# Three reorderings in a two-layer kernel: a copy ahead of the down scalings, weight sums in the order of the text, and one zero matmul fewer at the start

## The chip, the core and the metric

The kernel runs on one core of one Trainium2 chip. The metric is the device time of one execution in microseconds (us). A core has five engines with a queue of instructions each: TensorE (matmuls; PE in the profile, PEld for its weight loads), VectorE (DVE), ScalarE (ACT), GpSimd (POOL) and SyncE (SP), which here only issues DMAs. They wait for each other through semaphores.

## The reference, cut to what matters

```python
# x: (8, 256, 1024) f32; mask: (8, 1024, 1024) int32; coeff: (8,); W: (1024, 1024)
def first(x, W, b, coeff, mask):
    sign = 2 * mask - 1
    return einsum('bsi,oi->bso', x, W) + b + einsum('bsi,bio->bso', x, sign) * coeff[:, None, None]

def second(x, mapping, W, b, lora_As, lora_Bs):        # rank 16, SCALING = 2
    A, Bm = lora_As[mapping], lora_Bs[mapping]
    return einsum('bti,oi->bto', x, W) + b + einsum('btr,bro->bto', einsum('bti,bir->btr', x, A), Bm) * SCALING

x = x + first(x, W0, b0, coeff, mask)
x = x + second(x, W1, b1, mapping, lora_As, lora_Bs)
```

Every batch of the first layer has a weight of its own, W0 + coeff (2 mask - 1), and both residuals are put into the weights as an identity.

## The kernel before

Everything is held transposed: features on the 128 partitions, the 256 tokens of a batch along the free axis, in float32. The eight batches form two groups of four; each group goes through the first layer batch by batch and then through the second layer at once.

**Start.** `c_row`, the eight coefficients, is loaded by ScalarE's queue (L90). `idle(n)` (L98 to L100) issues n matmuls of zeros, which compute nothing that is used. `idle(2)` stands ahead of `spread` (L104), a matmul that copies the coefficients to all partitions (`c_ps`); `idle(3)` stands behind it. VectorE makes `two_c` and `neg_c` from `c_ps` (L108, L110). A float32 matmul shows as two matmuls in the profile.

**First layer.** A piece of mask is loaded by SyncE, ScalarE turns it into coeff (2 mask - 1) (`build`, L237) and VectorE adds W0 (L245). Batch 0 (L303) and batches 1 and 2 (L278) are plain products. Batches 3 to 7 (class `Seven`) multiply by blocks with seven products instead of eight (the Strassen-Winograd scheme): `token_sum` (L373) makes the sums t1 to t4 of the tokens, `weight_sum` (L356) the sums s1 to s4 of the weight blocks, each in two halves a = 0 and 1, `half` (L420) issues one half of a product, `with_bias` (L439, ScalarE) and `add` (L446, VectorE) read the results. For batch 3 the sums s3 and s4 are written over a weight block that has no other use left; other batches have a buffer for them. `operands` gives the order of the sums in the text: for each half s1 and then s2, then t3, s3, s4, t4. `products` gives the order of TensorE: X (a11), Y (a12), X (s2 with t2), Z (s1 with t1), X (s3 with t3), Z (s4), X (a22 with t4).

**Second layer.** The same seven-product scheme on two levels: `second_layer` runs seven outer products (`plan`), each of seven inner products (`product`, L722) whose weight operands ("leaves", `l_...`) are loaded by SyncE from DRAM, where GpSimd's queue has put them (`keep`, L534). `read` takes a product out of PSUM: ScalarE copies it (L776) where nothing is added, VectorE adds it (L778). The first outer product, `run(0, "A11", ...)`, has the adapters beside it: after its first two inner products `down` issues 64 small matmuls into `psh` (L757) and ScalarE scales the four batches' rows into `h_sb` (L766); later `up` multiplies `h_sb` by the adapters' rows into `G` (L740), which ScalarE copies (L750).

In group 0 the weight sums of the outer product S3 are made beside this: GpSimd's queue loads eight blocks again (`again`, L616), VectorE subtracts them (`outer`, L608) and makes the inner sums later (`inner_in_place`, L597).

**What sets the order.** A scheduler puts the instructions of each engine into an order of its own; the order of the text is only a wish. `tc.issue_after(i)` holds whatever is issued inside it behind instruction i. `behind(what)` does so with the last instruction that was noted in `anchors` under that name, and does nothing when none was noted. No order is given in `weight_sum` among the sums, nor in `down` between the scalings and the copy that `read` issues just ahead of it in the text.

Of the kernel before, what the change touches and what calls it, by code (L numbers as in the profile page):

```python
# [20 lines left out]
SCALING = 2.0  # L21
# [3 lines left out]
def kernel(  # L25
# [38 lines left out]
    nc = tc.nc  # L64
    B, NG, _, _, T = xT.shape
    R = lora_b.shape[1]
# [4 lines left out]
    GB = 4  # L71
    NGROUP = B // GB
    S = 32
# [21 lines left out]
    h_sb = const.tile([P, T], F32, tag="h", name="h_sb")  # L95
    idle_ps = psum.tile([P, T], F32, tag="ps", name="idle_ps")

    def idle(n: int):  # L98
        for _ in range(n):
            nc.tensor.matmul(idle_ps, lhsT=zeros[:, :P], rhs=zeros, start=True, stop=True)  # L100

    idle(2)
    c_ps = psum.tile([P, B], F32, tag="ps", name="c_ps")
    spread = nc.tensor.matmul(c_ps, lhsT=one_row, rhs=c_row, start=True, stop=True)  # L104
    with tc.issue_after(spread.ins):
# [31 lines left out]
    anchors = {}  # L137
# [6 lines left out]
    def behind(what: str):  # L144
        return tc.issue_after(anchors[what].ins) if what in anchors else nullcontext()
# [114 lines left out]
    def bank(name):  # L260
        return psum.tile([P, 2, T], F32, tag="ps", name=name)
# [67 lines left out]
    class Seven:  # L329
# [19 lines left out]
        def weight_sum(self, n, op, x, y, a):  # L349

            if self.b < GB and n in ("s3", "s4"):
                s = self.w[x, a]
            else:
                s = qpool.tile([P, CG, OH], F32, tag="q", name=f"{n}_{self.b}_{a}")
            self.w[n, a] = s
            anchors["weights"] = op(s, self.w[x, a], self.w[y, a])  # L356

        def tokens(self, c, v):

# [335 lines left out]
    def second_layer(group: int, y, first, first_steps, second):  # L695
# [3 lines left out]
        a = la_of[group]  # L699
# [52 lines left out]
        def down():  # L752
            ph = bank(f"psh_{group}")
            with behind("inner"):
                for c in range(NC):
                    for i in range(GB):
                        anchors["adapters"] = nc.tensor.matmul(  # L757
                            ph[i * S : i * S + R, 0, :],
                            lhsT=a[:, i, c, :],
                            rhs=y[i][c // TPH][:, c % TPH, :],  # L760
                            start=(c == 0),
                            stop=(c == NC - 1),
                        )
            for i in range(GB):
                rows = slice(i * S, i * S + R)
                nc.scalar.mul(h_sb[rows, :], ph[rows, 0, :], SCALING)  # L766

        banks = {}

# [142 lines left out]
        for _ in chain(islice(s3, 1), ordered(second.sums()), islice(t1, 2)):  # L912
# [4 lines left out]
            0, "A11", first, None, e1,  # L917
            beside=islice(s3, 4),
            early=down,
            mid=lambda: up(0, 0, lower),  # L920
            late=lambda: up(0, 1, lower),
# [67 lines left out]
    sums = iter(())  # L989
# [13 lines left out]
    for group in range(NGROUP):  # L1003
        y = [
            [
                ypool.tile([P, TPH, T], F32, tag=f"y{i}{h}", name=f"y_{GB * group + i}_{h}")
                for h in range(2)
            ]
            for i in range(GB)
        ]  # L1010
# [113 lines left out]
```

## Time and profile before

| what | value |
|---|---|
| three runs | 410.59, 412.04, 412.46 us (median 412.04) |
| profiled execution | 411.16 us, of which the span of instructions 409.5 us |
| granted TensorE clock | 1.00 of full speed |
| TensorE busy | 401.8 us, 98% of the span |
| VectorE busy | 312.5 us, 76% |
| ScalarE busy | 136.9 us, 33% |
| GpSimd busy | 52.1 us, 13% |
| moved by DMA | 99.56 MB, mean 243 GB/s |

A row of the page's groups names line, engine, operation, output<-input, shape and count, then busy time and the mean of one. A row of the timeline gives the start and the length in us, engine, line, operation, output<-input, shape and count; "[2.38 <-ACT e L776]" says that the engine stood idle for 2.38 us ahead of it until that instruction of ScalarE ended. Equal instructions that follow each other are one row. Names leave out buffer numbers, so an s3 sum of batch 3, written over a weight, reads "w<-w,w".

By stage the span divides about so: batch 0 to 2 of the first layer to 89.8 us, batch 3 to 115.8, the second layer of group 0 to 211.7, batches 4 to 7 to 312.3, and the second layer of group 1 to the end.

### The profile page before, as it was taken

How to read it: one execution, taken by the hardware profiler on the slowest of the kernel's cores; microseconds unless marked ns; L12 is line 12 of the kernel's file. 1: busy time of each engine (PE TensorE's matmuls, PEld its weight loads, DVE VectorE, ACT ScalarE, POOL GpSimd, SP SyncE). 2: the span in 40 equal slices, each digit the busy share in tenths (PEclk: the TensorE clock that was granted, in tenths of full speed). 3: DMA queues.
4: the chain of work that ended last, by engine and by line, in shares of the span. 5: the costliest groups of instructions: out<-in, count | busy, mean ns of one | idle time of the engine just before them, and what ended most of it. 6: DMA issues, size and time to landing. Idle time of an engine off the chain costs nothing.

```text
span 409.5 us, 6788 instructions
## 1 busy us (share of the span) xinstructions
PE 401.8 (98%) x2556; PEld 359.9 (88%) x2556; DVE 312.5 (76%) x446; ACT 136.9 (33%) x222; POOL 52.1 (13%) x102
## 2 busy tenths in 40 slices
PE   9999999999997999999999999999999999999996
PEld 7888888899976888888899999999998788888885
DVE  2437695989882579987999999999926247898593
ACT  4434525772115202223132926538221420102200
POOL 0000152106935021001040001200000000000000
PEclk9999999999999999999999999999999999999999
DMA  8999999980799699768799857831122247545644
GB/s 281 397 402 396 400 413 416 402 332 4 258 352 331 197 296 324 269 196 251 269 366 371 316 185 271 249 103 52 27 70 66 81 141 240 161 154 160 210 160 154
DMA packets 41540, 99.56 MB, mean 243 GB/s; under 512 B 5668, under 2 KB 6180, under 8 KB 41508
## 3 DMA queue, kind: packets, MB, share of 16 engines
q1 hardware_dynamic: 32834, 76.04, 54.0%
q0 software_dynamic: 6224, 18.90, 12.4%
q10 hardware_dynamic: 2450, 4.20, 2.8%
q8 instruction: 20, 0.33, 0.3%
q14 instruction: 12, 0.10, 0.1%
HBM read 79.19 MB, written 19.92 MB: 242 GB/s over the span
## 4 chain that ended last, share of the span: by engine, by line
PE 53%; issue 23%; DVE 10%; DMA 7%; POOL 6%; ACT 0%; SPq 0%; POOLq 0%; DVEq 0%
PE X L722 12%; PE ps L278 8%; PE X L420 8%; PE ps L303 7%; PE Z L722 6%; DVE s L356 4%; PE Z L420 3%; DVE w L245 3%; PE Y L722 3%; DMA x<-xT 2%; DMA w<-mask 2%; POOL outT L785 2%; DMA outT<-c 2%; PE Y L420 2%; DVE t L373 1%
## 5 line engine op out<-in xcount | busy, mean ns | idle before, releaser
L237 ACT ACTIVATE w<-w,neg_c,two_c 128x1024 f32<-128x1024 int32 (+1 forms) x68 | 79.0, 1195 | 63.6 <-DMA w<-mask 50.4
L245 DVE TENSOR_TENSOR w<-w,w_sb 128x1024 f32<-128x1024 f32 (+1 forms) x68 | 77.7, 1158 | 27.0 <-ACT w L237 22.0
L278 PE MATMUL ps<-x,w 128*128 128x256 f32 x256 | 55.4, 379 | 0.0
L278 PEld LDWEIGHTS ps<-x,w 128*128 128x128 f32 x256 | 48.6, 190 | 6.6
L439 ACT ACTIVATE y<-X,b_sb 128x128 f32<-128x128 f32 x60 | 17.2, 368 | 70.4 <-PE X L420 70.4
L420 PE MATMUL X<-t,s 128*128 128x128 f32 x288 | 34.1, 276 | 0.7 <-DVE s L356 0.7
L420 PEld LDWEIGHTS X<-t,s 128*128 128x128 f32 x288 | 33.0, 192 | 0.9 <-DVE s L356 0.9
L864 DVE TENSOR_TENSOR c<-c,e 128x512 f32<-128x512 f32 x48 | 31.9, 684 | 1.0 <-ACT c L750 1.0
L750 ACT COPY c<-G 128x512 f32<-128x512 f32 x32 | 16.4, 599 | 38.0 <-PE G L740 38.0
L303 PE MATMUL ps<-x,w 128*128 128x256 f32 x128 | 28.6, 386 | 0.0
L303 PEld LDWEIGHTS ps<-x,w 128*128 128x128 f32 x128 | 25.1, 196 | 3.7
L776 ACT COPY e<-X 128x512 f32<-128x512 f32 x16 | 9.4, 590 | 49.8 <-PE X L722 43.6
L778 DVE TENSOR_TENSOR c<-X,c 128x512 f32<-128x512 f32 (+1 forms) x26 | 16.7, 647 | 10.8 <-PE X L722 10.7
L420 PE MATMUL X<-t,w 128*128 128x128 f32 x192 | 22.5, 276 | 0.2 <-DVE y L446 0.2
L722 PE MATMUL X<-T_t,l_S_s 128*128 128x256 f32 x96 | 22.7, 379 | 0.0
L420 PEld LDWEIGHTS X<-t,w 128*128 128x128 f32 x192 | 21.9, 192 | 0.3 <-DVE y L446 0.3
L356 DVE TENSOR_TENSOR s<-w,w 128x1024 f32<-128x1024 f32 x18 | 21.6, 1218 | 0.0
L722 PEld LDWEIGHTS X<-T_t,l_S_s 128*128 128x128 f32 x96 | 18.2, 190 | 2.5
L420 PE MATMUL Z<-t,s 128*128 128x128 f32 x160 | 18.8, 275 | 0.0
L420 PE MATMUL Y<-x,w 128*128 128x128 f32 x160 | 18.7, 275 | 0.0
L420 PE MATMUL X<-x,w 128*128 128x128 f32 x160 | 18.7, 275 | 0.0
L420 PEld LDWEIGHTS X<-x,w 128*128 128x128 f32 x160 | 18.4, 192 | 0.1
(144 smaller groups left out, 658.8 us busy)
## 6 DMA issues: line engine op xcount, KB each, us to landing
w<-mask SPq DMA_DIRECT2D x60, 512.0 KB, 7.2
l_S_s<-leaf_S_s SPq DMA_DIRECT2D x32, 256.0 KB, 2.7
x<-xT SPq DMA_DIRECT2D x31, 256.0 KB, 6.6
l_A_s<-leaf_A_s SPq DMA_DIRECT2D x24, 256.0 KB, 3.0
l_S_a<-leaf_S_a SPq DMA_DIRECT2D x24, 256.0 KB, 3.2
w<-w1T SPq DMA_DIRECT2D x16, 256.0 KB, 7.2
outT<-c POOLq DMA_DIRECT2D x15, 256.0 KB, 5.6
outT<-c ACTq DMA_DIRECT2D x15, 256.0 KB, 2.7
```

The source lines that it names most:

```text
L237: nc.scalar.activation(w[:, i], m[:, i], AF.Identity, bias=neg_c[:, b : b + 1], scale=two_c[:, b : b + 1],)
L245: weff_at[k] = nc.vector.tensor_add(w[:, i], w[:, i], w0_of(k)[:, i])
L278: nc.tensor.matmul(ps[j // 2][:, j % 2, :], lhsT=w[:, c, j * P : (j + 1) * P], rhs=x_sb[b, g][:, c, :],  start=first and j % 2 == 0, stop= ...
L303: nc.tensor.matmul(ps[ot // 2][:, ot % 2, :], lhsT=w[:, h, j * P : (j + 1) * P], rhs=x_sb[0, c // CG][:, c % CG, :], start=c == 0 and ot % ...
L356: anchors["weights"] = op(s, self.w[x, a], self.w[y, a])
L420: anchors["products"] = nc.tensor.matmul(ps[:, j, :], lhsT=w[:, c, j * P : (j + 1) * P], rhs=r, start=first and a == 0 and c == 0 and j == ...
L439: sent = nc.scalar.activation(self.out(i, v)[:, j, :], ps[:, j, :], AF.Identity, bias=b0_sb[:, ot : ot + 1])
L722: anchors["inner"] = nc.tensor.matmul(ps[:, j, :], lhsT=l[:, c, j * P : (j + 1) * P], rhs=r[:, c, :], start=first and c == 0 and j == 0, s ...
L750: nc.scalar.copy(dest[b // 2][u, b % 2], ps[b])
L776: anchors["copies"] = nc.scalar.copy(out, ps)
L778: own["reads"] = anchors["reads"] = nc.vector.tensor_add(out, ps, other)
L864: nc.vector.tensor_add(o, o, x)
```

## The change

Three edits:

1. `idle(1)` instead of `idle(2)` ahead of `spread`.
2. In `weight_sum`, each sum is issued behind the one before it in the text, whichever batch it belongs to.
3. In `down`, the four scalings into `h_sb` are issued behind the last copy of `read`.

```diff
-    idle(2)
+    idle(1)
     c_ps = psum.tile([P, B], F32, tag="ps", name="c_ps")
     spread = nc.tensor.matmul(c_ps, lhsT=one_row, rhs=c_row, start=True, stop=True)
...
             self.w[n, a] = s
-            anchors["weights"] = op(s, self.w[x, a], self.w[y, a])
+            with behind("sums"):
+                anchors["weights"] = anchors["sums"] = op(s, self.w[x, a], self.w[y, a])
...
-            for i in range(GB):
-                rows = slice(i * S, i * S + R)
-                nc.scalar.mul(h_sb[rows, :], ph[rows, 0, :], SCALING)
+
+            with behind("copies"):
+                for i in range(GB):
+                    rows = slice(i * S, i * S + R)
+                    nc.scalar.mul(h_sb[rows, :], ph[rows, 0, :], SCALING)
```

In the order that the scheduler makes of this, four things differ from before. On TensorE one zero matmul is gone. On VectorE, in batch 3, the first half of s3 stands behind the second half of s2 and both halves of t3 instead of ahead of them. On ScalarE, in group 0, the copy of X's first reading stands ahead of the four scalings instead of behind them. And the four matmuls of `up` that first read `h_sb` in group 0 wait for the scalings by name, where the wait of X covered it. The orders of GpSimd and SyncE are the same, and so are batches 4 to 7 and group 1.

## The prediction

> **What bounds the kernel now.** I read the page's table of busy time first, then TensorE's list of waits, then the timeline around each wait on that list.
>
> ```profile
> PE 401.8 (98%) x2556; PEld 359.9 (88%) x2556; DVE 312.5 (76%) x446; ACT 136.9 (33%) x222; POOL 52.1 (13%) x102
> ```
>
> TensorE is busy for 401.8 of 409.5 us, so the kernel is TensorE's work plus 7.7 us in which it stands, and an edit that leaves its instructions alone can win no more than those. The waits of TensorE (total us, times, longest) say where they lie:
>
> ```profile
> PE X L722 <- ACT e L776: 2.4, 1, 2.4
> PE idle_ps L100 <- PEq L1113: 0.9, 1, 0.9
> PE X L420 <- DVE s L356: 0.7, 1, 0.7
> PE X L420 <- DVE y L446: 0.2, 1, 0.2
> ```
>
> The first and third row are what the diff touches. Timeline (start, length, engine, line) at the first row, group 0 of the second layer:
>
> ```profile
> 119.38 3.65 PE L757 MATMUL psh<-y,la 128*16 128x256 f32 x64
> ...
> 123.18 1.56 ACT L766 ACTIVATE h_sb<-psh 16x256 f32<-16x256 f32 x4 [6.00 <-PE psh L757]
> ...
> 124.76 0.59 ACT L776 COPY e<-X 128x512 f32<-128x512 f32 x1
> ...
> 125.40 1.99 PE L722 MATMUL X<-b_t,l_A_s 128*128 128x256 f32 x8 [2.38 <-ACT e L776]
> ```
>
> The copy reads a product that TensorE ended before 119.38. ScalarE has been free for 6.00 us, yet the copy stands behind four scalings that need the last down product. The same place in group 1 has the other order:
>
> ```profile
> 314.22 0.59 ACT L776 COPY e<-X 128x512 f32<-128x512 f32 x1 [0.58 <-PE X L722]
> ...
> 315.84 3.65 PE L757 MATMUL psh<-y,la 128*16 128x256 f32 x64
> ...
> 319.42 1.59 PEld L722 LDWEIGHTS X<-b_t,l_A_s 128*128 128x128 f32 x8 [0.42 <-issue]
> 319.42 1.99 PE L722 MATMUL X<-b_t,l_A_s 128*128 128x256 f32 x8
> 319.58 1.58 ACT L766 ACTIVATE h_sb<-psh 16x256 f32<-16x256 f32 x4 [4.77 <-PE psh L757]
> ```
>
> There X follows psh at once, while the scalings run: the kernel before already shows what group 0 will look like. The third row, batch 3 of the first layer, VectorE and then TensorE:
>
> ```profile
> 96.10 1.22 DVE L356 TENSOR_TENSOR s<-w,w 128x1024 f32<-128x1024 f32 x1
> 97.24 1.22 DVE L356 TENSOR_TENSOR w<-w,w 128x1024 f32<-128x1024 f32 x1
> 98.37 1.22 DVE L356 TENSOR_TENSOR s<-s,w 128x1024 f32<-128x1024 f32 x1
> ```
> ```profile
> 96.96 1.95 PE L420 MATMUL X<-t,s 128*128 128x128 f32 x16
> 99.65 2.05 PE L420 MATMUL X<-t,s 128*128 128x128 f32 x16 [0.74 <-DVE s L356]
> ```
>
> VectorE makes s1, then the s3 half (written over a weight, so "w<-w,w"), then the s2 half that TensorE waits for. And the start:
>
> ```profile
> 0.90 2.05 PE L100 MATMUL idle_ps<-const-float32-0.0 128*128 128x256 f32 x4 [0.90 <-PEq L1113]
> ...
> 2.88 0.59 PE L104 MATMUL c_ps<-c_row,one_row 1*128 1x8 f32 x2
> ...
> 4.73 0.69 DVE L245 TENSOR_TENSOR w<-w,w_sb 128x512 f32<-128x512 f32 x1 [0.99 <-DMA w_sb<-w0T]
> ```
>
> [...] the copy starts at 124.76, 0.02 us after the fourth scaling (123.18 + 1.56 = 124.74). [...] passes over 256 columns start 0.427 us apart up to 7.8 us and 0.216 us apart after it; one execution cannot show whether the moment varies.
>
> **Part 1: the copy ahead of the scalings (group 0).** The order of instructions of the changed kernel has this one move on ScalarE and none in group 1. From the start of psh to the start of X is 125.40 - 119.38 = 6.02 us in group 0 and 319.42 - 315.84 = 3.58 us in group 1: gain 2.44 us. The scalings cost nothing where they go: G (L740) reads them 3.65 us after X starts (125.40 to 129.05; group 1 has 319.42 to 323.07), they last 1.6 us, so about 2 us of X and Y hide them. Without that cover they would cost up to those 1.6 us. The new wait of the copy, for X's first product, is over before psh begins, and behind it on ScalarE stand only the scalings. What is late next: VectorE. From 121.8 to 130.28 it waits 8.47 us for the S3 loads that GpSimd issues (A<-w1T), and behind that sum in its order stands the reading of Y at 130.89, another S3 sum at 131.49, an addition at 132.09 and the reading of Z at 132.79 to 133.48. TensorE's next use of Z is at 136.58, 3.10 us later. Moving up by 3.47 us (the sum below) it comes at 133.11. If the loads land as now, the reading of Z ends about 133.37 (an addition at its usual 0.60 us step after 132.09), and TensorE waits 133.42 - 133.11 = 0.31 us. But GpSimd's loads follow VectorE's S4 sums (L597, 118.94), which part 2 brings forward by about 1 us, so I cost this wait at nothing and keep 0.31 us for the range. I take 2.44, bounds 2.1 and 2.5.
>
> **Part 2: s2 before the s3 half (batch 3).** Only this sum moves on VectorE, by an s2 half and the two t3 subtractions; batches 4 to 7 keep their order. Sixteen passes take 1.785 us (Y at 93.39 to X at 96.96 is 3.57 for 32), so the second X could start at 96.96 + 1.785 = 98.75 instead of 99.65: 0.90 us. VectorE after: s1 ends at 97.32, s2 needs it (dependent sums in this trace start 0.03 us after the end) and runs 97.35 to 98.57, TensorE can go at 98.62, 0.13 us before it gets there. The s3 half then runs about 99.2 to 100.4; TensorE wants it at 105.11, some 4 us off even after the shift. The reading of Y, 100.18, becomes 0.1 us later and has no hurry; at 108.95 VectorE waits 1.48 us for TensorE, which is where the shift passes on to it. Value 0.90. Bounds: 0 where TensorE reaches this point late anyway, 1.03 where it comes early.
>
> **Part 3: one zero matmul fewer.** It is two passes, 2 x 0.427 = 0.85 us of cold TensorE. c_row has landed at 2.07 (the wait of TensorE's sequencer ends there), so c_ps starts near 2.15, not 2.88: 0.72 us earlier, and with it neg_c and the three zero matmuls behind. The first weights do not come sooner: VectorE's sum at 4.73 is released by w0T, and ends at 5.42. So the first real matmul moves from 6.12 only to about 5.63 (5.42, and 0.2 us to load weights into an idle array), 0.49 us. These run at half clock up to 7.8, worth half: 0.25 us. TensorE then has 0.53 us or more over each weight to 89.8, so 0.25 survives to batch 3, but there s2 is the limit: the masks feeding it come at DMA pace (busy share 1.03 from 7.76 to 89.80), not TensorE's. Of 0.25 only the 0.13 above counts. Bounds: [...] above, 0.4.
>
> **Sum.** 2.44 + 0.90 + 0.13 = 3.47 us. It carries to the end because later waits are relative: leaf loads and masks are issued when TensorE frees a buffer, the leaf loads are issued some 7 us ahead of use (150.69 for X at 157.41) and land 2.3 us or more ahead, and VectorE, full from 195 to 262 us, is released at 194.69 by TensorE (1.03 us wait). The profiled execution took 411.16 us (span 409.5 and 1.66 around it): 411.16 - 3.47 = 407.69. The median of the runs, 412.04, lies 0.88 higher: **408.6 us**.
>
> **Rivals.** (a) Only the copy pays: in most runs TensorE comes to batch 3 later than in the profiled one, so there is no 0.90 to win. For it: the median is 0.88 over the profiled run; against: nothing in the trace. 412.04 - 2.44 = 409.6. (b) [...] (c) Nothing measurable: what moves up is eaten by waits of runs that the profile didn't catch, or the reorder does not act; the built order speaks against the latter: 411 to 412. (d) Slower: with TensorE ahead, its leaf loads meet GpSimd's eight S3 loads (256 KB each, 3.6 to 7.8 us to landing) and these land later by d than now. VectorE stands in order behind them and TensorE waits 0.31 + d at Z. Gain gone at d = 3.47 - 0.31 = 3.16 us, and 0.5% slower from 5.2 us; at 5.5 us, 412.04 + 0.31 + 5.5 - 3.47 = 414.4. Against: at most four leaf loads of 256 KB come forward.
>
> **How the numbers follow.** Forecast 0.70, (a) 0.13, (b) 0.07, (c) 0.07, (d) 0.03. About 0.5% (2.06 us, bound 409.98) is what a measurement of this kernel tells from no change. Forecast and (a) lie below the bound but for the scatter of medians (the three runs spread 1.87 us): 0.67 + 0.11, and 0.02 of (b): faster 0.80; slower is (d), 0.03; the rest 0.17. Range: below, 408.6 - 0.4 for part 3's upper bound and 1 us of scatter, 407.2; above, (a) at 409.6 and most of (b), 410.4.
>
> **What would show it.** Part 1: the first row is gone from TensorE's waits, e<-X of group 0 starts before psh ends. Part 2: 0.74 gone at the second X<-t,s, whose start is 1.8 us after the first's. Part 3: c_ps near 2.2 us, first L303 near 5.6, spacing of 0.216 from about 7.8. Wrong if a new wait of TensorE on VectorE's e (L778) shows near 133 us, if the cold spacing lasts past 8 us, or if batch 3 still waits.

## The result, and the profile after

The changed kernel takes 408.69 us (median of 6 runs, 408.10 to 409.15), the kernel before 411.46 us beside it (6 runs, 410.59 to 412.46): ratio 0.9931, 95% interval 0.9909 to 0.9952. The profiled executions took 411.16 before and 408.34 after, 2.82 us less. The experiments below add 82 more runs of the kernel before in three series of 35, 35 and 12, with medians 411.41, 411.18 and 412.25.

The page's table of busy time of the changed kernel has the same work, less the zero matmul's two passes:

```profile
PE 401.1 (99%) x2554; PEld 359.7 (88%) x2554; DVE 312.3 (77%) x446; ACT 136.8 (34%) x222; POOL 51.9 (13%) x102
```

TensorE's list of waits:

```profile
PE idle_ps L100 <- PEq L1116: 0.9, 1, 0.9
PE Z L723 <- DVE e L781: 0.5, 1, 0.5
PE c_ps L104 <- DMA c_row<-coeff: 0.4, 1, 0.4
```

The 2.4 us for the copy and the 0.7 us at batch 3 are gone. Two rows are new: Z waits for VectorE, and `c_ps` for its coefficients. The timeline of the changed kernel in group 0, ScalarE and TensorE (start, length):

```profile
116.85 0.58 ACT L779 COPY e<-X 128x512 f32<-128x512 f32 x1 [0.59 <-PE X L723]
...
118.47 3.65 PE L758 MATMUL psh<-y,la 128*16 128x256 f32 x64
...
122.04 2.00 PE L723 MATMUL X<-b_t,l_A_s 128*128 128x256 f32 x8
...
122.27 1.57 ACT L769 ACTIVATE h_sb<-psh 16x256 f32<-16x256 f32 x4 [4.83 <-PE psh L758]
```

The copy is done before psh begins, X starts 3.57 us after psh (6.02 before), and the scalings run beside X: part 1 as forecast, 2.45 us. Batch 3, VectorE and TensorE:

```profile
97.03 1.23 DVE L357 TENSOR_TENSOR s<-s,w 128x1024 f32<-128x1024 f32 x1
...
97.05 3.74 PE L421 MATMUL X<-t,s 128*128 128x128 f32 x32
...
98.84 1.22 DVE L357 TENSOR_TENSOR w<-w,w 128x1024 f32<-128x1024 f32 x1
```

The s2 half now runs ahead of the s3 half, and the 32 passes of X are one row without a break. Its second sixteen follow at 97.05 + 1.785 = 98.84 us instead of 99.65: 0.81 us earlier, and 0.90 less between the first pass and the seventeenth (1.79 us against 2.69). The start:

```profile
2.54 0.56 PE L104 MATMUL c_ps<-c_row,one_row 1*128 1x8 f32 x2 [0.45 <-DMA c_row<-coeff]
...
4.88 0.69 DVE L245 TENSOR_TENSOR w<-w,w_sb 128x512 f32<-128x512 f32 x1 [1.50 <-DMA w_sb<-w0T]
...
5.75 10.50 PE L303 MATMUL ps<-x,w 128*128 128x256 f32 x42
```

The first real matmul moved from 6.12 to 5.75, but the records of the clock have full speed from 8.29 us instead of 7.76, and by 8.3 us TensorE was 0.09 us behind the kernel before. Now the new wait at Z: VectorE and TensorE, with GpSimd's first and last group of S3 loads:

```profile
121.79 0.55 POOL L617 DMA_DIRECT2D A<-leaf_A_a  x1
...
123.94 2.16 POOL L617 DMA_DIRECT2D A<-w1T  x4
...
130.61 0.69 DVE L609 TENSOR_TENSOR A<-A,A 128x512 f32<-128x512 f32 x1 [9.71 <-DMA A<-w1T]
...
131.22 0.68 DVE L781 TENSOR_TENSOR e<-Y,e 128x512 f32<-128x512 f32 x1
...
131.82 0.68 DVE L609 TENSOR_TENSOR A<-A,A 128x512 f32<-128x512 f32 x1
...
132.42 0.69 DVE L867 TENSOR_TENSOR c<-c,e 128x512 f32<-128x512 f32 x1
...
133.02 0.69 DVE L781 TENSOR_TENSOR e<-Z,e 128x512 f32<-128x512 f32 x1
...
133.76 2.00 PE L723 MATMUL Z<-y,l_A_s 128*128 128x256 f32 x8 [0.47 <-DVE e L781]
```

The same place in the kernel before:

```profile
122.69 0.55 POOL L616 DMA_DIRECT2D A<-leaf_A_a  x1
...
130.28 0.69 DVE L608 TENSOR_TENSOR A<-A,A 128x512 f32<-128x512 f32 x1 [8.47 <-DMA A<-w1T]
...
136.58 1.99 PE L722 MATMUL Z<-y,l_A_s 128*128 128x256 f32 x8
```

The loads are issued 0.90 us earlier than before (121.79 against 122.69), yet the first S3 sum starts at 130.61 instead of 130.28. In VectorE's order Y's and Z's readings stand behind it: Y ended at 125.76 (123.87 + 1.89), its reading starts at 131.22, 0.61 us after the sum, and TensorE stands 0.47 us before Z. The shift against the kernel before is 0.81 to 0.91 after batch 3, 3.36 at X of group 0, 2.82 at Z, and 2.82 from there to the end.

### The profile page after: what moved, and what is told of

The parts are those of the page before. It is cut to its first block, busy times and chain, and to the rows that moved or that the text cites. A ratio compares the mean times of both kernels' runs of the same rounds, so it can differ in the third digit from the quotient of the medians.

```text
span 406.7 us, 6785 instructions
## 1 busy us (share of the span) xinstructions
PE 401.1 (99%) x2554; PEld 359.7 (88%) x2554; DVE 312.3 (77%) x446; ACT 136.8 (34%) x222; POOL 51.9 (13%) x102
## 4 chain that ended last, share of the span: by engine, by line
PE 62%; issue 20%; DVE 9%; POOL 4%; DMA 4%; POOLq 0%; DVEq 0%
PE ps L278 14%; PE X L723 12%; PE X L421 11%; PE ps L303 7%; PE Z L723 6%; PE Z L421 4%; DVE s L357 3%; DVE w L245 3%; PE Y L723 3%; PE Y L421 3%; POOL outT L788 2%; DMA outT<-c 2%; DMA leaf_A_s<-A_s 2%; DVE t L374 1%; PE G L741 1%
```

## The experiments

Theory after the comparison: the copy is worth 2.45 us less about 0.5 at Z, the sums 0.9, the zero nothing. Rivals: the sums' gain is swallowed at Z; the zero matters through the clock; the wait at Z comes from full DMA engines, and no reordering on VectorE takes it away.

**e1_copy_only.** Part 1 alone:

```diff
-            for i in range(GB):
+            with behind("copies"):
+                for i in range(GB):
...
```

> The kernel before with only the copy ahead of the scalings. Theory (the parts add up, and the new wait at Z comes from S3 loads that share full DMA engines): X of group 0 starts 3.58 us after psh instead of 6.02, gain 2.44; the S3 loads are issued as late as before (122.7) but meet earlier leaf loads, so the first S3 sum comes 0.3 to 1.2 us later than before's 130.28, and TensorE waits 0 to 0.5 us at Z: net gain 2.0 to 2.4 us. Rival (landing of the S3 loads scatters by itself): first S3 sum at 130.3, no wait at Z, gain 2.4. Rival (only the copy pays in the changed kernel): gain 2.8, as much as the whole change.

Measured: 408.78 (408.31 to 409.52), ratio 0.9937 (0.9916 to 0.9958), before 411.41. That is 2.63 us by the medians, though its trace has the same picture as the changed kernel's: 2.44 us won at X and 0.60 lost at Z, so 1.84. Some 0.8 us was not in the trace of before.

**e2_sums_only.** Part 2 alone:

```diff
-            anchors["weights"] = op(s, self.w[x, a], self.w[y, a])
+            with behind("sums"):
+                anchors["weights"] = anchors["sums"] = op(s, self.w[x, a], self.w[y, a])
```

> The kernel before with only the order of the weight sums. Theory: the wait of 0.74 us at the second X<-t,s is gone, its start is 1.8 us after the first's, gain 0.9 in the profiled execution and carried to the end; the S3 loads and the leaf loads both move up by 0.9, the first S3 sum comes near 129.4. Rival (only the copy pays): 0.0 to 0.3 us.

Measured: 410.70 (409.56 to 412.05, 22 runs), ratio 0.9979 (0.9966 to 0.9992): 0.71 us. TensorE's list of waits:

```profile
PE X L723 <- ACT e L777: 2.4, 1, 2.4
PE idle_ps L100 <- PEq L1114: 0.9, 1, 0.9
PE X L421 <- DVE y L447: 0.2, 1, 0.2
```

The wait at batch 3 is gone, the one for the copy is still 2.4 us, and there is none at Z.

**e3_zero_only.** Part 3 alone:

```diff
-    idle(2)
+    idle(1)
```

> The kernel before with one zero matmul fewer. Theory: c_ps earlier by 0.3 to 0.7 us, first real matmul by 0.3 to 0.5 us, but the moment of full clock decides how much of that stays, and batch 3 waits for VectorE anyway: gain 0.0 plus or minus 0.2 us, the wait at batch 3 grows by what is gained before. [...]

Measured: 411.56 (410.17 to 415.00, 14 runs), ratio 1.0000 (0.9982 to 1.0017): nothing. Its profile happened to catch the longest run, 415.0 us, and showed what the other traces didn't. The timeline of TensorE behind the copy's wait, and the busy times of one stretch there (us, then PE, PEld, DVE, ACT, POOL busy, granted clock, DMA share, GB/s):

```profile
121.66 3.65 PE L757 MATMUL psh<-y,la 128*16 128x256 f32 x64
127.68 3.55 PE L722 MATMUL X<-b_t,l_A_s 128*128 128x256 f32 x8 [2.38 <-ACT e L776]
131.06 1.89 PE L722 MATMUL Y<-y,l_A_a 128*128 128x256 f32 x8
```
```profile
127.50:130.80 3.30, 3.12 (x7) 2.50 (x8) 0.00 (x0) 0.13 (x1) 1.80 (x4) 0.50 1.00 319
```

X's eight passes take 3.55 us instead of 1.99, at a clock of 0.50: the records have half clock from 127.44 for 3.41 us. The stand of 2.38 us (the time in which TensorE waits there) was followed by a stretch of half clock, and so cost 1.56 us more than itself. That gave a new theory for the 0.8 us: the 411.41 of the kernel before is a middle of two groups of runs. Of the 35 beside e1, e2 and e3 19 lie from 410.25 to 411.71 and 16 from 412.02 to 413.28; e2, which keeps the copy's wait, has two groups too, 409.56 to 410.44 and 410.96 to 412.05; the kernels without that wait (e1 408.31 to 409.52, the changed kernel 408.10 to 409.15) have one.

**e9_wait_filled.** It tests that: TensorE's stand is filled with work that is not used, and nothing is made shorter.

```diff
+            if group == 0:
+                fill = bank("fill")
+                with behind("adapters"):
+                    for _ in range(5):
+                        anchors["adapters"] = nc.tensor.matmul(
+                            fill[:, 0, :], lhsT=zeros[:, :P], rhs=zeros, start=True, stop=True
+                        )
             for i in range(GB):
```

> The kernel before with one addition: in group 0, between psh and X, TensorE gets five matmuls of zeros (ten passes of 256 columns, about 2.2 us at 0.216 us each) that compute nothing that is used. They end at about 125.2 us, ahead of the copy's end at 125.4, so TensorE waits for the copy only some 0.2 us more, and X starts when it did before. What changes is that the 2.4 us stand is now busy. Theory (the stand sometimes costs the clock: half clock for about 3.4 us after it, 1.5 us lost, in about half of the executions): the runs gather near the lower half of the runs of the kernel before, 410.3 to 411.4, and 412 or more is hardly seen; median about 410.8, 0.5 to 0.8 below before. Rival (the scatter of before has nothing to do with that stand): the runs scatter as those of before do, in two clusters 1.5 us apart, median 411.4 within 0.3.

Measured: 410.83 (410.37 to 411.96, 22 runs), ratio 0.9983 (0.9972 to 0.9993); 20 of the 22 lie below 411.4, while of the 35 of before beside it 18 lie at or below 411.18 and 17 at or above 411.95. TensorE's timeline:

```profile
119.02 3.65 PE L757 MATMUL psh<-y,la 128*16 128x256 f32 x64
122.59 2.44 PE L768 MATMUL fill<-const-float32-0.0 128*128 128x256 f32 x10
125.03 1.99 PE L722 MATMUL X<-b_t,l_A_s 128*128 128x256 f32 x8
```

From psh to X it is 6.01 us, as before (6.02), and the upper group is gone. Work that computes nothing made the kernel faster: the theory holds, the rival falls.

The mean clock of every run is on record too, and shows it directly. One stretch of 3.41 us at half clock takes 3.41 x 0.5 / 411 = 0.004 off the mean; e3's profiled run has 0.996. Of the 82 runs of before, the 41 at 411.95 us or above all have 0.994 to 0.996, and the 41 at 411.71 or below all have 0.998 or more. Of all 118 runs that keep the stand (before, e2, e3) 58 have 0.996 or less; of the 91 in which it is filled or gone, none has. The two slowest of e9, 411.80 and 411.96, ran at 1.00, so their cause is another one.

In e9 the first S3 sums also moved behind Y's reading on VectorE, which touches no wait of TensorE in the kernel before.

**e8_s3_sums_behind_reads.** The changed kernel with the S3 sums two steps later, which on VectorE puts the readings of Y and Z ahead of them:

```diff
-            beside=islice(s3, 4),
+            beside=chain((None, None), islice(s3, 4)),
```

> The changed kernel with the first S3 sums of group 0 behind the readings of Y and Z on VectorE, loads as they are. Theory: TensorE's wait of 0.47 us at Z comes from VectorE's order, which puts the readings behind sums that wait for the S3 loads; it goes, the time falls by about 0.5 us below the changed kernel to 408.2, if the sums find room later. Rival (TensorE's gain of 0.5 is taken back elsewhere, since VectorE has the same work to do): the wait at Z goes, but another of the same size comes within the next 15 us, same time as the changed kernel.

Measured: 407.79 (407.38 to 409.72), ratio 0.9920 (0.9895 to 0.9944). Timeline of VectorE and TensorE:

```profile
125.45 0.69 DVE L781 TENSOR_TENSOR e<-Y,e 128x512 f32<-128x512 f32 x1 [4.98 <-PE Y L723]
...
129.01 0.69 DVE L781 TENSOR_TENSOR e<-Z,e 128x512 f32<-128x512 f32 x1 [1.26 <-ACT e L779]
...
130.50 0.69 DVE L609 TENSOR_TENSOR A<-A,A 128x512 f32<-128x512 f32 x1 [0.80 <-DMA A<-w1T]
...
132.80 1.99 PE L723 MATMUL Z<-y,l_A_s 128*128 128x256 f32 x8
```

The S3 sum starts as late as in the changed kernel (130.50), but nothing that TensorE wants stands behind it.

**e8b_reads_first_zero_kept.** The same with `idle(2)`, so without part 3.

> The changed kernel with the S3 sums of group 0 two steps later beside the first outer product, so that the readings of Y and Z stand ahead of them on VectorE (that one ran at 407.79), and with the zero matmul of part 3 put back. Theory (the zero is worth nothing: c_row's landing, the sum at 5.4 us and a clock that comes up at its own moment decide the start): 407.8 within 0.3. Rival (it is worth the 0.25 us at the start that the prediction worked out, or the 0.13 it counted): 408.0 to 408.1[...].

Measured: 407.68 (407.61 to 409.80), ratio 0.9906 (0.9880 to 0.9933), against 407.79 without the zero, which ran on another chip: part 3 is again worth nothing that can be measured.

**e5_s3_loads_ahead_of_stores.** The changed kernel with the S3 loads on GpSimd's queue ahead of S4's stores:

```diff
+            self.read(8)
...
-        for _ in chain(islice(s3, 1), ordered(second.sums()), islice(t1, 2)):
+        for _ in chain(ordered(second.sums()), islice(t1, 2)):
...
+            def loads_of_s3():
+                next(later["S3"])
+                sums_of("S4")
...
-                3: lambda: sums_of("S4"),
+                8: loads_of_s3,
```

> The changed kernel with the first pair of S3's loads issued on GpSimd's queue ahead of S4's stores instead of behind them; VectorE's first two S3 sums then also stand behind the reading of Y. Theory (the new wait at Z comes from S3 sums that stand in VectorE's order ahead of the readings and wait for loads): the wait of TensorE at Z, 0.5 us in the changed kernel, is gone, and the time is about 0.5 below the changed kernel's: 408.1, range 407.6 to 408.5. Rival (the DMA engines are full from 116 to 134 us, so what is issued earlier only makes other transfers land later, masks or leaves): a wait of TensorE shows for a leaf or for another sum, and the time stays at 408.7 or above.

Measured: 407.58 (407.03 to 408.08), ratio 0.9894 (0.9871 to 0.9916). Timeline of GpSimd, VectorE and TensorE:

```profile
115.78 0.55 POOL L618 DMA_DIRECT2D A<-leaf_A_a  x1 [1.48 <-DMA leaf_A_s<-A_s]
...
125.54 0.69 DVE L782 TENSOR_TENSOR e<-Y,e 128x512 f32<-128x512 f32 x1 [4.97 <-PE Y L724]
...
126.52 1.49 DVE L610 TENSOR_TENSOR A<-A,A 128x512 f32<-128x512 f32 x2 [0.29 <-DMA A<-w1T]
...
129.10 0.69 DVE L782 TENSOR_TENSOR e<-Z,e 128x512 f32<-128x512 f32 x1 [0.48 <-ACT e L780]
...
132.89 1.99 PE L724 MATMUL Z<-y,l_A_s 128*128 128x256 f32 x8
```

The loads go out at 115.78, the sums run from 126.52, and Z waits for nothing. No wait comes in its place: TensorE's list has only the 0.2 us at batch 3 that the kernel before has too, and the start. So the rival of full DMA engines falls as a limit. From the first issue to the first sum it is 10.74 us here, though, against 8.82 in the changed kernel: issued 6.01 us earlier, the loads served their sum 4.09 us earlier. S4's stores, now last, show in no wait of TensorE. VectorE's order moved too (Y's reading is ahead of the sums now), so e5 alone does not tell which of the two took the wait away; e8, which moved the sums alone, does.

**e6_scalings_three_times.** It measures the cover that the prediction gave the scalings:

```diff
-                for i in range(GB):
+                for i in [*range(GB)] * 3:
```

> The changed kernel with each of the four scalings issued three times in both groups (12 instead of 4, 4.7 us instead of 1.57; the output is the same). It measures the cover that the prediction gave them: X and Y, 3.65 us between the start of X and G. Theory: the scalings end about 4.9 us after the start of X, so G waits about 1.3 us in group 0 and about 1.2 in group 1, and the stand in group 0 takes in the 0.5 us that Z waited for: slower than the changed kernel by 2.0 to 2.5 us, 410.7 to 411.2. Rival (G's wait lets nothing through because later waits swallow it, or TensorE does G's share later): within 0.5 us of the changed kernel. A second rival, the cover is smaller than worked out (ScalarE's copies stand behind the scalings and are wanted sooner than G): slower by over 3 us, with a wait on ScalarE's e rather than on h_sb.

Measured: 410.49 (409.54 to 411.18, 14 runs), ratio 0.9963 (0.9950 to 0.9976). Timeline:

```profile
121.70 1.99 PE L723 MATMUL X<-b_t,l_A_s 128*128 128x256 f32 x8
...
121.92 4.77 ACT L769 ACTIVATE h_sb<-psh 16x256 f32<-16x256 f32 x12 [4.83 <-PE psh L758]
...
125.59 2.28 PE L741 MATMUL G<-h_sb,lb_pad 32*128 32x256 f32 x16 [0.17 <-issue]
...
127.80 1.99 PE L723 MATMUL X<-b_t,l_A_s 128*128 128x256 f32 x8
```

The same place in the changed kernel, behind its X at 122.04:

```profile
125.69 1.15 PE L741 MATMUL G<-h_sb,lb_pad 32*128 32x256 f32 x16
126.77 1.99 PE L723 MATMUL X<-b_t,l_A_s 128*128 128x256 f32 x8
```

From X to the X behind G it is 6.10 us instead of 4.73 (122.04 to 126.77), 1.37 more, and in group 1 6.04 instead of 4.73, 1.31 more. Most of it hides inside the row of G, whose 16 passes take 2.28 us instead of 1.15, as each batch's matmuls wait for their own scaling; the list of waits shows 0.2. Less the 0.5 us at Z, which this stand takes in, that is 2.2 us; the medians and the profiled executions differ by 1.8, a little under the 2.0 to 2.5 expected. The eight scalings more take 3.20 us, of which 1.31 to 1.37 show, so the cover is real and about as long as worked out: 1.8 to 1.9 us beyond the scalings' 1.57.

**Do the parts add up?** The copy alone (408.78) and all parts (408.69) had come out almost equal, so four kernels ran beside each other on one chip: with and without the sums, with and without the wait at Z, the zero kept in all.

> The copy ahead of the scalings alone, a second time, as the base of the three kernels beside it on the same chip. It ran at 408.78, the changed kernel with all three parts at 408.69, though the sums alone were worth 0.7 to 0.9 us in the run by themselves. Expected here: 408.8, range 408.3 to 409.3.

> The copy and the sums, without part 3 (the zero matmul is kept). Against the copy alone this measures what the sums are worth on top of it. Theory A (parts add up; the two runs so far merely scattered): 0.7 to 0.9 below the copy alone, 408.0. Theory B (the gain of the sums comes to batch 3 but is swallowed at Z in group 0, where TensorE waits for an S3 sum that follows its loads and these do not come sooner by the same amount): within 0.3 of the copy alone, 408.6. In theory B the wait at Z in the profile is longer than with the copy alone, in theory A it is the same 0.5 to 0.6.

> The copy ahead of the scalings and the S3 sums two steps later, so that there is no wait at Z; the sums of batch 3 in the old order, the zero matmul kept. Both theories expect about 0.5 below the copy alone: 408.3. Against the next kernel, which adds the sums, theory A and B both expect the sums to be worth 0.6 to 0.9 here, as nothing swallows them.

> The copy, the sums and the S3 sums two steps later, the zero matmul kept, a second time beside the others: 407.7, range 407.3 to 408.0. The four kernels together give the sums' worth with the wait at Z (second minus first) and without it (fourth minus third), and the worth of taking the wait at Z away without the sums (third minus first) and with them (fourth minus second).

Measured (6 or 7 runs each, before 412.25 in 12 runs):

| us, ratio to before (95%) | sums as before | sums in order |
|---|---|---|
| S3 sums ahead of the readings | 409.53 (e1 again), 0.9931 (0.9906 to 0.9955) | 408.41 (e3b), 0.9917 (0.9892 to 0.9941) |
| S3 sums behind them | 408.45 (e10), 0.9925 (0.9899 to 0.9952) | 407.36 (e8b again), 0.9893 (0.9869 to 0.9918) |

The sums are worth 1.12 us with the wait at Z and 1.09 without it; taking the wait away is worth 1.08 and 1.05. The wait at Z is the same with the sums as without, 0.7 us in e3b and 0.6 in e1 again:

```profile
PE Z L723 <- DVE e L781: 0.7, 1, 0.7
```

So the differences and the wait speak for theory A, and the swallowing at Z falls. The times themselves missed: e1 again was expected at 408.3 to 409.3, and e3b came between the 408.0 of theory A and the 408.6 of theory B. The near equality of the first two numbers was scatter, between executions or between chips, and the intervals of neighbours in the table still overlap.

What scatters is seen at batch 3. Waits of TensorE in the second run of the copy alone:

```profile
PE X L420 <- DVE s L356: 0.9, 1, 0.9
PE Z L722 <- DVE e L779: 0.6, 1, 0.6
```

In the first profile of the same kernel the wait at batch 3 was too short to be listed. VectorE's s1 half started at 95.48 us there and at 96.44 here, X at 96.93 and 97.13: TensorE and VectorE come to this point at moments of their own, so the sums were worth from about 0.3 to 1.1 us from execution to execution.

## Why the prediction was right, and where its steps were not

The time predicted was 408.6 and 408.69 was measured. The sum behind it was 3.47 us, and the two profiled executions differ by 2.82. Of the three signs of being wrong that the prediction named, two showed: TensorE waits for VectorE's e at 133.76 us, and the cold spacing (0.427 us from pass to pass) lasts past 8 us, to 8.29. Only batch 3 no longer waits. So the two larger parts were right, two smaller steps were wrong, and that the time fits so closely is in part luck, as the sum further down shows.

- **Part 1, 2.44 us at X: right, in size and cause.** 2.45 in the trace, and the scalings lie under X and Y as said; e6 measured that cover.
- **Part 2, 0.90: right.** 0.81 to 0.91 in the trace, 0.7 to 1.1 in the runs. That it would hang on who comes first was in its bounds, 0 to 1.03. In e9's profile the wait there is 1.13 us, but the bound is on the gain: its s2 half starts at 98.02, and could start at most about 1.02 us sooner, behind the end of s1 at 96.97 (an estimate from that trace).
- **Part 3, 0.13: too much, by little.** In two comparisons the kernel without the zero took 0.15 us (e3) and 0.11 us (e8 and e8b, on two chips) more, which is nothing. That `c_ps` would start near 2.15 held in four of the five profiles without the zero (2.17 to 2.29), but not in the changed kernel's (2.54): there TensorE stands 0.45 us ahead of it, where the kernel before has no stand. Also the first weight came 0.15 us later (VectorE's sum at 4.88 instead of 4.73; the first real pass is 0.18 us behind its end at 5.57), and the clock came up 0.53 later. Rival (b) was a later full clock, at a price that was the author's estimate and that no trace showed; e3's profile alone has full clock past 8.3 us, at 11.39.
- **The wait at Z, "so I cost this wait at nothing": wrong.** The reason given was that GpSimd's loads would be issued about 1 us sooner. They were, by 0.90, but took 8.82 us from the first issue to the first sum instead of 7.59. The formula of rival (d) was right: with d = 130.61 - 130.28 = 0.33 it gives 0.31 + 0.33 = 0.64 us at a shift of 3.47, so 0.53 at the 3.36 that there was, and Z lost 0.54. The later landing of rival (d) came, 0.33 us of it, a tenth of the d that it needed to make the kernel slower. The longer way goes with the copy's edit: from first issue to first sum it is 7.45 to 8.36 us in the four profiles in which X starts 6 us behind psh (before, e2, e3, e9), and 8.82 to 10.27 in the nine in which it starts 3.6 us behind psh and the loads keep their place in the queue. That it comes from DMA engines that are full is only argued: their busy share from 116 to 134 us is 0.96 before and 0.99 after. The trace of before held a warning: with a share of 0.96, nothing in it showed that an issue 0.90 us earlier would land 0.90 us earlier.
- **The base.** 412.04 was the middle of three runs of a kernel whose runs fall into two groups. Pooled, 41 of 82 lie at or below 411.71 and 41 at or above 411.95, and in the two series of 35 the medians of the groups lie 1.4 us apart. The profiled execution, 411.16, was of the lower group, and the prediction counted the 0.88 us between the two as scatter that the changed kernel would have too. It was mostly the stretch at half clock, which goes away with the wait for the copy.

So 408.6 is close because errors went in opposite directions. The base, 412.04, was 0.58 us above the 411.46 beside the changed kernel, and the gain, 3.47, was 0.70 above the 2.77 by the medians. Counted from the profiled executions: the 0.88 us should not have been added, against a gain 0.65 too large and a profiled execution of the changed kernel (408.34) that is 0.35 below its own median.

What the copy wins on top of its wait, the stretch at half clock, is worth by this account 1.56 us in about half of the executions, 0.8 on average; with 2.44 - 0.60 that makes 2.64, and the copy alone measured 2.63 and 2.72 (medians of a kernel with two groups are a coarse measure). With all parts this account gives 2.82 + 0.8 = 3.6 us for the changed kernel, and 2.8 was measured, with an interval of 2.0 to 3.7. The missing 0.8 lies between the profiled executions and the other runs: 411.16 is 0.41 above the middle of the three lower runs of before in that comparison (410.59, 410.75, 410.88), and 408.34 is 0.35 below the median of the changed kernel. Why executions of one group differ by that much, no run shows. The kernel without part 3, e3b, measured 3.8, its lower end 2.4.

Of the rivals, (a), (b) and (c) are out as the likely course: the sums pay (e2, e3b), one zero less cost nothing on average (e3, ratio 1.0000), and the gain is above what runs can hide. The versions with the copy and the sums and without the wait at Z (e8, e8b, e8b again, e5) measured below both kernels: 407.36 to 407.79, with ratios of 0.9893 to 0.9920 to before; against the kernel with copy and sums it is 1.05 us less beside it, with overlapping intervals, and only 0.5 to 0.7 of this is the wait in the traces; the rest is open. Single runs of e8, e8b and e10 lay at 409.7 to 410.0, some 2 us above their others, with no wait for the copy; their clock is 0.998 to 0.999, so it is not that stretch of half clock. No profile caught one, and their cause stays open too.

## What to carry to other kernels

When a wait is removed, follow the instruction that is late next through its whole queue: here a sum on VectorE that waits for a load held up a reading that TensorE wanted, and moving the sum, not the load, was enough. A load that is issued earlier should not be booked as landing earlier by as much: here, at a busy share of the DMA engines of 0.96 to 0.99, 0.90 us earlier brought nothing, and 6.01 us earlier brought 4.09 (e5). A wait in TensorE can cost more than its length (2.38 us and 1.56 more in e3's profile), so its worth is read from several runs of the kernel before and their mean clock, not from one trace.

## What the hardware showed that was not expected

**A stand of 2.38 us can be followed by half clock.** 3.41 us of half clock followed it in e3's profile, but not in those of before and e2, whose stands were as long. The clock records show one more thing: the stretches of full clock between the first and the last change of clock, 116.05 us in e3, 399.36 in the changed kernel and 402.77 in before, are 34, 117 and 118 times 3.413 us, the length of e3's half-clock stretch. Counted on in steps of that length from the moment of full clock (an estimate from these records), a step ended at 127.44 in e3, where half clock began, and 2.13 us of the stand lay inside it (psh's end at 125.31 to 127.44). In before a step's end at 123.81 cuts the stand into 0.78 and 1.59, in e2 one at 122.59 cuts it into 1.17 and 1.21. So the one stand with 2.13 us inside one step was followed by half clock, and the two with at most 1.59 were not; three profiles make no rule of it. That the stand makes the upper group is shown by e9 and by the clock of every run: 58 of 118 runs with it have a mean clock of 0.996 or less, none of the 91 without.

**The moment of full clock varies by more than 3 us.** With the zero kept it was 7.76, 7.69, 6.54, 7.05, 6.49, 7.89, 6.70, 4.87 and 4.69 us after the first instruction, without it 8.29, 6.47, 7.85, 7.85 and 11.39. With values as spread as these, fourteen profiles do not tell whether the zero matmul moves it.
